# Moving six sums and differences of a 3x3 convolution's first two groups from VectorE to GpSimd

## The chip, the cores and the metric

The kernel runs on one core of one Trainium2 chip. A core has engines that run side by side, each through its own queue of instructions in order: TensorE (PE) multiplies matrices into PSUM, VectorE (DVE) and ScalarE (ACT) work element by element and can read PSUM, GpSimd (POOL) works element by element on SBUF, and SyncE (SP) issues transfers; ACT and GpSimd issue some transfers too. Engines wait for one another through semaphores. The metric is the device time of one execution in microseconds, less is better.

## The reference

Two bottleneck blocks, one after the other, on an input of 64 images of 1024 channels and 14 by 14 pixels, all in fp32:

```python
out = jax.nn.relu(_bn(_conv(x, w1, b1, 1, 0), g1, be1))      # 1x1, 1024 -> 256
out = jax.nn.relu(_bn(_conv(out, w2, b2, 1, 1), g2, be2))    # 3x3, 256 -> 256
out = _bn(_conv(out, w3, b3, 1, 0), g3, be3)                 # 1x1, 256 -> 1024
out = jax.nn.softplus(residual_scale)[0] * out
return jax.nn.relu(x + out)
```

Batch norm takes mean and variance over all 64 images, so each convolution must be finished before its result can be normalized.

## The kernel before

The 256 channels between the convolutions lie in one SBUF tile, `y_all`, for all images; `y_grp` is a view of it by groups of 8 images. The 1x1 convolutions use a fast matrix multiplication with seven products in place of eight. Each block has one 3x3 stage (`conv2`), and the change is in it alone. In the profile these stages lie at about 305 to 560 us and 1258 to 1540 us.

The 3x3 stage works through `NG` = 8 groups of 8 images. Within a group the 14 rows are cut in `RT` = 4 tiles of 4 output rows (the last tile has 2), and each tile of rows is computed from `NF` = 6 products by a fast convolution along the rows, made in pairs in the order (1, 2), (3, 4), (5, 0). I number these products 0 to 47 through a stage, six to a group. Per product the work is:

- DVE makes combinations of input rows, `steps` and `r`, and from each of them the column sums, differences and steps `sums`, `diffs`, `v` (`combine`, `Inputs`, lines 667, 681, 689, 760 to 784, and 636 for every multiply-and-add).
- TensorE multiplies them with transformed filters: `m` from the sums, `l` from the differences, and even and odd `columns` from the steps (line 175).
- ACT copies `m` into both halves of the `columns` bank pair before TensorE adds its columns to them (`put`, lines 844, 846, or 338 where the order is written out; below: the fill), and `l` into the SBUF tile `ls` (`bring`, line 866 or 338).
- DVE adds `columns` and `ls` into a tile `f` (`add_to`, line 885; below: the eviction).

TensorE's order in step k is: `l` of k, even columns of k, `m` of k + 1, odd columns of k. There are two `columns` bank pairs of PSUM, so the fill of product k + 1 waits for the eviction of product k - 1, and the even columns of k + 1 wait for that fill.

`finish` makes the output rows from the six evictions of a group. From the first two it makes the sum `a` (tile `fa`) and the difference `d` (tile `fb`); from the next two the sum `c` (tile `fc`) and the difference `e`, written over the older of the two `f` tiles. ACT copies the last row of each from `a` and `d` into `y` (lines 939 and 946). The inner rows come from these four by multiply-and-adds on DVE (line 636, written `y<-f,fb` where it reads `e` and `d`, and `y<-fc,fa`), the first of the outer rows by an add on DVE (line 938). For groups 0 to 5 the remaining evictions, 4 and 5 of the group, are added to the output rows by transfers from GpSimd's queue (lines 965, 966 and 982); until those have landed, their `f` tiles stay taken. There are three `f` tiles and one each of `fa`, `fb`, `fc`.

A planner orders the instructions of each engine by its own estimates, except those passed to `keep_in_program_order` (TensorE's all are; ACT's are where `act` is called). So a changed engine can change the order of other instructions on DVE and ACT. In the compiled program of the changed kernel TensorE's and SyncE's orders are the same as before; DVE's and ACT's differ inside the 3x3 stages.

Of the kernel before, what the change touches and what calls it, by code (L numbers as in the profile page):

```python
# [90 lines left out]
def bottlenecks(ctx: ExitStack, tc: tile.TileContext, x, w1s, w2s, w3s, pars, out):  # L91
    nc = tc.nc
# [501 lines left out]
    def conv2(b, par, aff, early, rest):  # L594
# [32 lines left out]
        def new(tag, tiles=RT):  # L627
            v = place(tag, MS * RT * LINE)
            return v[:, : MS * tiles * LINE].rearrange("p (s r l) -> p s r l", s=MS, r=tiles)
# [5 lines left out]
        def stt(to, a, by, c):  # L635
            return nc.vector.scalar_tensor_tensor(to, a, by, c, ALU.mult, ALU.add)
# [253 lines left out]
        def halves(f):  # L890

            return f.rearrange("p o r (i q c) -> p q (o r i) c", i=GI, q=2)

        def outputs(c):
            return c.add_to(new("f", c.lines // GI))

        def finish():


            for g in range(NG):  # L900
                out_rows = [y_grp[:, :, g, k::4, :] for k in range(4)]
                last_group = g == NG - 1

                by_transfer = g < NG - 2

                def stat(k, lines):
                    if last_group:
                        for o in range(MS):
                            nc.vector.bn_stats(stats[:, o, 1 + k, :], lines[o])

                ca = yield
                fa = outputs(ca)
                if g == 1:
                    begin(y_grp[:, :, 0, 1 : 4 * full : 4, :])
                fb = outputs((yield))
                a, d = new("fa"), new("fb")
                nc.vector.tensor_add(a, fa, fb)
                nc.vector.tensor_sub(d, fa, fb)

                fa = outputs((yield))  # L920
                fb = outputs((yield))
                c, e = new("fc", full), fa
                nc.vector.tensor_add(c, fa, fb)
                nc.vector.tensor_sub(e, fa, fb)
                a3, d3 = (v[:, :, :full] for v in (a, d))
                end = y_grp[:, :, g, H - 1]

                def middle_rows():

                    for o in range(MS):  # L930
                        stt(out_rows[1][:, o, :full], e[:, o], 2.0, d3[:, o])
                        stt(out_rows[2][:, o], c[:, o], 4.0, a3[:, o])

                def outer_rows():

                    if by_transfer:

                        nc.vector.tensor_add(out_rows[0][:, :, :full], a3, c)
                        nc.scalar.activation(out_rows[0][:, :, full], a[:, :, full], AF.Copy)
                    else:  # L940
                        nc.vector.tensor_add(a3, a3, c)
                    if by_transfer:

                        for o in range(MS):
                            stt(out_rows[3][:, o], e[:, o], 8.0, d3[:, o])
                        nc.scalar.activation(end, d[:, :, full], AF.Copy)
                    else:
                        stt(d3, e, 8.0, d3)

                if g > 1:  # L950
                    middle_rows()
                    outer_rows()
                if last_group:
                    for o in range(MS):
                        lines = y_grp[:, o, g, 1 : 1 + 4 * full].rearrange("p (r k) l -> p r k l", k=4)[:, :, :2]
                        for k in range(2):
                            moment(lines, idle[:, : 2 * full * LINE].rearrange("p (r k l) -> p r k l", k=2, l=LINE), o, k, g)

                fa = outputs((yield))
                if g < 2:  # L960
                    outer_rows()

                if by_transfer:
                    for o in range(MS):
                        nc.gpsimd.dma_start(out=out_rows[3][:, o], in_=fa[:, o, :full], accum_op=ALU.add)
                    nc.gpsimd.dma_start(out=end, in_=fa[:, :, full], accum_op=ALU.add)
                else:
                    nc.vector.tensor_add(out_rows[3], d3, fa[:, :, :full])
                    nc.vector.tensor_add(end, d[:, :, full], fa[:, :, full])
                stat(0, [out_rows[3][:, o] for o in range(MS)])  # L970
                stat(1, [end[:, o] for o in range(MS)])
                if last_group:
                    merge()

                cb = yield
                if g < 2:
                    middle_rows()
                if by_transfer:

                    f = outputs(cb)  # L980
                    for o in range(MS):
                        nc.gpsimd.dma_start(out=out_rows[0][:, o], in_=f[:, o], accum_op=ALU.add)
                    continue
                nc.vector.tensor_add(halves(a), halves(a), cb.by_columns(cb.ls))
                for j, q in enumerate((EVEN, ODD)):
                    for o in range(MS):
                        to, more = (
                            v[:, o].rearrange("p r (i q c) -> p q r i c", i=GI, q=2)[:, q] for v in (out_rows[0], a)
                        )
                        nc.vector.tensor_add(to, cb.banks[:, q, o].rearrange("p (r i c) -> p r i c", r=RT, c=WH), more)  # L990
                    stat(2 + j, [out_rows[0][:, o].rearrange("p r (i q c) -> p q r i c", i=GI, q=2)[:, q] for o in range(MS)])
            yield
# [8 lines left out]
        def begin(lines):  # L1001

            for o in range(MS):
                act(idle[:, : full * LINE].rearrange("p (r l) -> p r l", l=LINE), lines[:, o], AF.Identity,
                    scale=-1.0 / (full * LINE), accum_out=center[:, o : o + 1])

        def moment(y, to, o, k, g):
            act(to, y, (AF.Identity, AF.Square)[k], bias=center[:, o : o + 1], accum_out=moments[:, o, k, g : g + 1])

        def merge():  # L1010

            n = GPX * (NG - 1) + 2 * full * LINE
            m = small.tile([P, MS, 2], FP, tag="m12", name="m12")
            for o in range(MS):
                nc.vector.tensor_reduce(m[:, o], moments[:, o], mybir.AxisListType.X, ALU.add)
            eng = nc.gpsimd
            eng.tensor_scalar(m, m, 1.0 / n, None, ALU.mult)
            var = small.tile([P, MS], FP, tag="m12var", name="m12var")
            eng.tensor_tensor(var, m[:, :, 0], m[:, :, 0], ALU.mult)
            eng.tensor_sub(var, m[:, :, 1], var)  # L1020
            eng.tensor_sub(m[:, :, 0], m[:, :, 0], center)

            for half in range(2):
                to = stats[:, :, 0, 3 * half : 3 * half + 3]
                eng.memset(to[:, :, 0], n / 2)
                eng.tensor_copy(to[:, :, 1], m[:, :, 0])
                eng.tensor_scalar(to[:, :, 2], var, n / 2, None, ALU.mult)
# [29 lines left out]
        for _ in first_combination(inputs, 0, t):  # L1057
            pass
        coming, finished = items(), finish()
        next(finished)  # L1060

# [674 lines left out]
```

## Time and profile before

| what | us |
|---|---|
| median of three runs (1921.5 to 1921.92) | 1921.75 |
| the profiled execution | 1921.91 |
| its span, first to last instruction | 1920.1 |
| TensorE busy | 1902.8 |
| DVE busy | 1544.7 |
| ACT busy | 1086.5 |
| GpSimd busy | 564.6 |
| one of the 16 sums `fa`, or differences `fb`, 128 x 896, on DVE | 1.09 |
| one of the 16 sums `fc`, or differences in an `f` tile, 128 x 672, on DVE | 0.85 |
| DVE busy between 305 and 353 us, 48 us | 47.34 |

Times in profile lines are microseconds from the span's start. In a line of the timeline the first number is the start, the second the duration, then come the engine, the line of the kernel, the operation, the output and input tiles and their sizes; brackets give the idle time of the engine before the instruction and what ended it. Consecutive instructions on DVE overlap by some 0.08 us in the records. The stages are not alike: what an engine is worth in the 3x3 stage is read there and not from its share of the whole span.

### The profile page before, as it was taken

To read this page: it belongs to the slowest core of one execution; us is meant where nothing else is said; L and a number is where in the kernel's file an instruction comes from. 1 tells how busy PE (TensorE), PEld (TensorE's weight loads), DVE (VectorE), ACT (ScalarE), POOL (GpSimd) and SP (SyncE) were. 2 spreads that over 40 slices of the span, in tenths; PEclk is the share of its full clock that TensorE was granted. 3 is DMA by queue.
4 is the path that set the end of the run, shared out by engine and by line. 5 is a ranking of instruction groups with operands and counts; after the bars stand their busy time and mean duration, and the time that the engine had idled before them with its cause. 6 is when DMAs were issued, how large, how long until landed. Compare 5 with 4: busy or idle time off the path is not lost.

```text
span 1920.1 us, 28731 instructions
## 1 busy us (share of the span) xinstructions
PE 1902.8 (99%) x10236; PEld 1598.6 (83%) x10236; DVE 1544.7 (80%) x2499; ACT 1086.5 (57%) x2160; POOL 564.6 (29%) x678
## 2 busy tenths in 40 slices
PE   9999999999999999999999999999999999999999
PEld 5555557999998799999999999989999987555555
DVE  5787767999998866676776767789999986888886
ACT  2222214677778255555555555556777682666666
POOL 0111100211204133433433333302121041666664
PEclk9999999999999999999999999999999999999999
DMA  7767644887856544444444444358878466899998
GB/s 291 272 245 272 221 156 154 204 214 212 215 169 172 193 159 169 169 168 181 178 180 168 168 169 178 124 179 208 213 207 223 141 171 243 291 325 346 328 338 303
DMA packets 198527, 408.77 MB, mean 213 GB/s; under 512 B 37104, under 2 KB 175024, under 8 KB 181872
## 3 DMA queue, kind: packets, MB, share of 16 engines
q1 hardware_dynamic: 159712, 321.85, 48.9%
q0 software_dynamic: 33056, 34.03, 8.5%
q10 hardware_dynamic: 5616, 51.06, 6.4%
q8 instruction: 81, 1.33, 0.3%
q14 instruction: 62, 0.51, 0.1%
HBM read 263.75 MB, written 115.34 MB: 197 GB/s over the span
## 4 chain that ended last, share of the span: by engine, by line
PE 87%; issue 5%; DVE 3%; DMA 2%; POOL 2%; ACT 1%; SPq 0%; DVEq 0%; POOLq 0%; ACTq 0%
PE cy L175 17%; PE ay L175 14%; PE columns L175 14%; PE cp L175 11%; PE ap L175 8%; PE m L175 7%; PE l L175 6%; PE cx L175 5%; PE ax L175 4%; PE ps L175 1%; POOL home L1186 1%; POOL u L222 1%; DMA home<-y 1%; DVE zt L1223 0%; DMA u<-y 0%
## 5 line engine op out<-in xcount | busy, mean ns | idle before, releaser
L338 ACT ACTIVATE cu<-cy,scale 128x196 f32<-128x196 f32 (+1 forms) x552 | 256.3, 473 | 278.1 <-PE cy L175 272.9
L175 PE MATMUL columns<-v,ub 128*128 128x224 f32 (+1 forms) x1536 | 302.6, 339 | 4.8 <-ACT columns L846 3.9
L338 ACT ACTIVATE x<-x,shift 128x392 f32<-128x392 f32 x452 | 255.0, 613 | 73.1 <-POOL x L530 53.9
L175 PEld LDWEIGHTS columns<-v,ub 128*128 128x128 f32 x1536 | 269.0, 189 | 10.8 <-ACT columns L846 5.8
L504 DVE SCALAR_TENSOR_TENSOR x<-cp,scale,x 128x196 f32<-128x196 f32 (+1 forms) x368 | 178.3, 484 | 96.4 <-PE cp L175 95.2
L175 PE MATMUL cy<-ct,ws 128*128 128x196 f32 (+1 forms) x736 | 222.0, 383 | 1.2 <-ACT cu L338 1.2
L175 PE MATMUL ay<-at,ws 128*128 128x196 f32 (+1 forms) x768 | 212.9, 382 | 0.0
L525 POOL TENSOR_TENSOR x<-x,cu 128x196 f32<-128x196 f32 (+1 forms) x184 | 159.6, 867 | 171.6 <-ACT cu L338 163.8
L530 POOL TENSOR_TENSOR x<-x,cu 128x392 f32<-128x392 f32 x124 | 125.8, 1014 | 191.8 <-DVE x L504 186.9
L175 PEld LDWEIGHTS ay<-at,ws 128*128 128x128 f32 x768 | 139.5, 190 | 34.7 <-ACT au L338 0.6
L175 PEld LDWEIGHTS cy<-ct,ws 128*128 128x128 f32 x736 | 133.6, 190 | 36.2 <-ACT cu L338 3.7
L175 PE MATMUL l<-diffs,ub 128*128 128x224 f32 (+1 forms) x768 | 149.6, 337 | 0.3 <-ACT sd L1478 0.3
L551 POOL TENSOR_TENSOR x<-x,cu 128x392 f32<-128x392 f32 x120 | 121.9, 1016 | 86.4 <-DVE x L504 63.0
L175 PE MATMUL m<-sums,ua 128*128 128x224 f32 (+1 forms) x752 | 146.0, 337 | 0.2 <-DVE sums L667 0.2
L338 ACT ACTIVATE au<-ay 128x196 f32<-128x196 f32 (+1 forms) x140 | 53.3, 381 | 147.9 <-PE ay L175 145.4
L175 PEld LDWEIGHTS l<-diffs,ub 128*128 128x128 f32 x768 | 134.7, 190 | 1.1 <-ACT sd L1478 0.6
L504 DVE SCALAR_TENSOR_TENSOR x<-cx,scale,x 128x196 f32<-128x196 f32 (+1 forms) x184 | 89.1, 484 | 56.7 <-PE cx L175 56.5
L175 PEld LDWEIGHTS m<-sums,ua 128*128 128x128 f32 x752 | 131.5, 190 | 1.3 <-DVE sums L667 0.7
L175 PE MATMUL cy<-y,w 128*128 128x196 f32 (+1 forms) x408 | 125.4, 394 | 0.0
L175 PE MATMUL cx<-y,w 128*128 128x196 f32 (+1 forms) x400 | 122.7, 392 | 0.0
L175 PE MATMUL cp<-y,ws 128*128 128x196 f32 (+1 forms) x368 | 113.6, 391 | 0.1
L175 PE MATMUL cy<-ct,w 128*128 128x196 f32 (+1 forms) x368 | 111.0, 383 | 0.5 <-ACT cu L338 0.5
(238 smaller groups left out, 3915.2 us busy)
## 6 DMA issues: line engine op xcount, KB each, us to landing
x<-in_x SPq DMA_DIRECT2D x62, 1568.0 KB, 6.9
ub<-u SPq DMA_DIRECT2D x92, 768.0 KB, 5.4
x<-mid SPq DMA_DIRECT2D x32, 1568.0 KB, 7.9
mid<-x ACTq DMA_DIRECT2D x31, 1568.0 KB, 5.1
out<-x SPq DMA_DIRECT2D x123, 392.0 KB, 5.6
ua<-u SPq DMA_DIRECT2D x92, 256.0 KB, 3.0
u<-y POOLq DMA_DIRECT2D x48, 256.0 KB, 6.2
home<-y SPq DMA_DIRECT2D x70, 96.0 KB, 3.6
```

Of the source, the lines that this page charges most:

```text
L175: tc.keep_in_program_order(nc.tensor.matmul(*args, **kw))
L222: nc.gpsimd.dma_start(out=us[b][i][:, s, o], in_=u)
L338: tc.keep_in_program_order(nc.scalar.activation(*args, **kw))
L504: nc.vector.scalar_tensor_tensor(v, bank, self.scale[:, o : o + 1], v, ALU.mult, ALU.add)
L525: nc.gpsimd.tensor_add(self.part(1, 1), self.part(1, 1), u3)
L530: nc.gpsimd.tensor_add(v, v, self.u12)
L551: nc.gpsimd.tensor_add(v, v, self.u12[:, i * self.n : (i + 1) * self.n])
L1186: ins = queue.dma_start(out=x[32 * i : 32 * i + 32, :, j], in_=y_all[32 * j : 32 * j + 32, :, a + i * run : a + i * run + run])
```

## The change

In group 0 the sum `a`, the difference `d`, the sum `c` and the difference `e` are computed by GpSimd instead of DVE; in group 1 only `c` and `e` are. All other groups are as before. The stage is run once per block, so twelve instructions move.

```diff
                 fb = outputs((yield))
                 a, d = new("fa"), new("fb")
-                nc.vector.tensor_add(a, fa, fb)
-                nc.vector.tensor_sub(d, fa, fb)
+                eng = nc.vector if g else nc.gpsimd
+                eng.tensor_add(a, fa, fb)
+                eng.tensor_sub(d, fa, fb)

                 fa = outputs((yield))
                 fb = outputs((yield))
                 c, e = new("fc", full), fa
-                nc.vector.tensor_add(c, fa, fb)
-                nc.vector.tensor_sub(e, fa, fb)
+                eng = nc.vector if g > 1 else nc.gpsimd
+                eng.tensor_add(c, fa, fb)
+                eng.tensor_sub(e, fa, fb)
```

## The prediction

> **What bounds the kernel now.** I read the page's busy times first:
>
> ```profile
> PE 1902.8 (99%) x10236; PEld 1598.6 (83%) x10236; DVE 1544.7 (80%) x2499; ACT 1086.5 (57%) x2160; POOL 564.6 (29%) x678
> ```
>
> TensorE is busy 99% of the span, so a shorter vector queue can win only where TensorE waits for it. Next I asked what TensorE waited for in the first two groups of each 3x3 stage, 290 to 420 us and 1280 to 1410 us:
>
> ```profile
> PE columns L175 <- ACT columns L846: 1.6, 2, 1.1
> ...
> PE columns L175 <- ACT columns L846: 1.9, 2, 1.4
> ```
>
> Two waits in each block, 3.5 us in all: that is all there is to win here. The timelines of DVE, ACT and TensorE show what is late:
>
> ```profile
> 351.06 2.09 DVE L885 TENSOR_TENSOR f<-columns,ls 128x896 f32<-128x896 f32 x2
> ...
> 352.24 1.09 ACT L846 ACTIVATE columns<-m 128x448 f32<-128x448 f32 x2 [2.44 <-DVE f L885]
> ...
> 353.38 1.81 PE L175 MATMUL columns<-v,ub 128*128 128x224 f32 x8 [1.08 <-ACT columns L846]
> ```
>
> [...]Eviction 5 (first of the two at 351.06) frees the bank pair that ACT fills for product 7, and TensorE waits 1.08 us for that. The same happens 34 us later with eviction 11 (0.55 us), and in block 1 (1.38 and 0.55 us). The eviction's data had lain ready for 6.5 us (odd columns 5 end at 344.5): DVE is behind. From 314 to 356 us DVE never idles, so each us added to or taken from its queue ahead of eviction 5 moves that eviction by a us.
>
> Whether GpSimd takes the work off DVE without harm is read where both work today, in the 1x1 stages:
>
> ```profile
> 1007.27 0.60 POOL L525 TENSOR_TENSOR x<-x,cu 128x196 f32<-128x196 f32 x1
> 1009.14 1.35 POOL L525 TENSOR_TENSOR x<-x,cu 128x196 f32<-128x196 f32 x1 [1.27 <-ACT cu L338]
> ...
> 1009.05 0.97 DVE L456 TENSOR_TENSOR at<-x,at 128x784 f32<-128x784 f32 x1 [1.24 <-PE ay L175]
> ...
> 1641.24 1.13 POOL L525 TENSOR_TENSOR x<-x,cu 128x392 f32<-128x392 f32 x1
> ...
> 1641.42 1.37 DVE L470 TENSOR_TENSOR ct<-y 128x392 f32<-128x392 f32 x1
> 1642.71 0.55 DVE L468 TENSOR_TENSOR ct<-y 128x392 f32<-128x392 f32 x1
> ```
>
> The same GpSimd add takes 0.60 us alone and 1.35 us when it starts 0.09 us into a DVE add of two SBUF tiles; it ends 0.47 us (its own 0.60 less 0.13) after DVE's add. The other way round, DVE's L470 takes 1.37 us behind a running GpSimd add where its twin L468 takes 0.55; it really begins 0.13 us before GpSimd's end. They take turns.
>
> [...]this trace has 600 ns for 196 and 1015 for 392, or 0.185 us + 2.12 ns an element. At the sizes moved that is 2.08 us (896) and 1.61 us (672), estimates[...].
>
> **The change part by part, block 0.** In each block six instructions leave DVE: a and d of group 0 (896), c and e of groups 0 and 1 (672). Start to start these cost DVE 1.00 and 0.77 us (325.65 to 326.65; 335.39 to 336.16), so group 0 is relieved by 2.00 + 1.54 = 3.54 us, group 1 by 1.54.
>
> They reappear on GpSimd, which was idle there (34 us before 341.10), but beside two-SBUF adds. Which of two waiting engines gets the port between back-to-back DVE adds this trace doesn't show: I take alternation. Then, with the compiled order of the changed kernel:
> - Eviction 1 ends at 324.96 and a is released; DVE's r (324.88 to 325.73) holds the port, so a ends at 325.73 + 1.95 = 327.68. DVE's next, sums, begins at 327.55 and not 325.65: 1.9 us late. d ends 1.95 after sums (328.64), at 330.59, and DVE's diffs loses 1.9 us more.
> - Eviction 3 releases c. DVE's sums is ahead of it (1.0 us); c ends 1.48 us after that (2.48 after the eviction). DVE's next, the sum into y (L938), waits for c, and the one after it (L636, y from e) waits for e, which queues behind c and contends with L938. That one starts about 4.9 us after the eviction, where sums and L938 alone would have ended after 1.7: 3.2 us late.
>
> So DVE loses 1.9 + 1.9 + 3.2 = 7.0 us and is spared 3.54: it is 3.5 us later at eviction 5, which goes to about 354.5, and TensorE's columns 7 go from 353.38 to 356.9.
>
> An ACT queue effect lies under this. ACT runs in order, and the new order puts both last-row copies (L939 reading a, L946 reading d) ahead of the fill of the bank pair for product 3. Today:
>
> ```profile
> 326.83 0.39 ACT L939 ACTIVATE y<-fa 128x224 f32<-128x224 f32 x1
> 327.12 0.90 ACT L338 ACTIVATE columns<-m 128x336 f32<-128x336 f32 x2
> ```
>
> L946 can't start before d ends at 330.59, so the fill runs 330.95 to 331.85 and TensorE's columns 3, today at 328.52, start at 331.9: a 3.4 us stall. It doesn't add to the 3.5: TensorE, 3.4 late, would reach columns 7 at 355.7, and DVE's 356.9 decides.
>
> Group 1 adds 3.2 and spares 1.54 (+1.7), but now uses up the 1.84 us for which DVE waits for TensorE before eviction 7 (at 357.99). Eviction 11: 3.5 + 1.7 - 1.8, 3.4 us late, taken as 3.3 with roundings. TensorE alone would be 3.5 late less the vanished wait of 0.55. So block 0 ends 3.3 us later.
>
> **Block 1.** The order differs: only L939 lies inside the fill of product 3 (one half before it, one after), L946 is ahead of fill 4. a ends at 1278.76 + 1.95 = 1280.7, today's L939 starts at 1280.82: no stall there. DVE loses the same 7.0 us, is spared 3.54; ACT's fill for product 7 is no longer split by an ls copy (0.3 us gained), and DVE's wait in group 1 is 2.17 us. Together 3.5 + 1.7 - 2.2 = 3.0 us.
>
> From group 2 on no instruction moves engine. DVE's order differs slightly and reaches in group 3 the order that the kernel before has from group 5, where TensorE doesn't wait: 0. GpSimd's queue: the transfers of row 3 (L965, L966) stand behind c and e, but wait for evictions 4 and 10 anyway (347.6 and later), after e: 0. They land 3 to 7 us after issue, before eviction 6 (358) wants their buffer, just; if not, up to 1 us more a block. The sync queue and TensorE's order are unchanged. In the copy of e into the old f tile one wait is added, for c: counted above.
>
> Sum: 3.3 + 3.0 = 6.3 us. The profiled execution took 1921.91 us (span 1920.1, 1.8 us around it), 0.16 above the median of 1921.75: 1928.2 on its scale, **1928.0** on the median's.
>
> **Bounds of the unknown.** If GpSimd gets the port only when DVE pauses or evicts, d ends after eviction 2 (about 333.1 in block 0): fill 3 ends at 334.4, a stall of 5.9 us. DVE itself loses 0.9 less, so TensorE decides, and the vanished waits of 1.08 and 0.55 come off: block 0 is 4.3 late, block 1 about 2: again 6.3. If even the short pause between dependent adds doesn't let it in, a waits for eviction 2 and d for eviction 3, and the blocks are about 8 and 3 late.
>
> **Rivals.**
> 1. *No blocking in this stage*: the 1x1 lines don't carry over, GpSimd runs beside DVE. Then DVE is early and the four waits for evictions 5 and 11 (1.08 + 0.55 + 1.38 + 0.55 = 3.56 us) go. In block 0, a and d still end at 327.1 and 329.2, L946 holds fill 3 until 330.5, 2.0 us of stall. Net -3.56 + 2.0 = -1.6: 1920.1. This is the one on the other side; it decides once less than 3.5 of the 7.0 us of DVE's losses are real. Against it: every overlap of such adds in the trace shows the block. 0.12, of which 0.03 beyond 0.2% (the stall at fill 3 missing too: 1918.2).
> 2. *Half hidden*: GpSimd's adds fall more beside evictions and DVE's waits than I laid them, lateness about 1.5 us a block: 1924.8. For it: evictions take 5.5 of a group's 33 us[...]. 0.16.
> 3. *Starved GpSimd*, as bounded above: L946 in ACT's queue makes columns 3 very late. 11 us: 1932.7. Against: dependent adds leave some 0.1 us between them. 0.12.
> 4. My forecast, 4 to 8.5 us slower: 0.60. Its own range is 1925.7 to 1930.2.
>
> That the change does nothing is out: GpSimd's compiled queue has 12 instructions more.
>
> **Range and chances.** 0.2% (3.8 us) is about what can be told from no change. Slower: 0.60 + 0.12 = 0.72; same: 0.16 + 0.09 = 0.25; faster 0.03. From 1921.5 (leaves out most of rival 1) to 1932.5 (half of rival 3).
>
> **What would show it.** GpSimd's rows of 896 elements at 2.1 us alone, near 2.7 to 4 with waits; DVE's sums and diffs in group 0 near 3 us instead of 1.09; ACT waiting for GpSimd before L939 and L946; TensorE's wait before columns 3 of block 0 of about 3.4 us, and none in block 1; waits for fill 7 still there. If DVE's adds keep 1.09 us, rival 1 holds. Wrong also if TensorE waits in groups 2 to 7, which I put at nothing.

## The result, and the profile after

The changed kernel takes 1936.41 us (five runs, 1935.57 to 1937.44) against 1921.75 us (five runs by then, 1921.5 to 1921.92): a ratio of 1.0077 with a 95% interval of 1.0067 to 1.0088. It is slower by 14.7 us. The forecast was 1928.0 us with a range up to 1932.5: the direction was right, the size was less than half of what came.

The page's busy times of the changed kernel show first that no engine became the bound:

```profile
PE 1906.0 (99%) x10236; PEld 1597.6 (83%) x10236; DVE 1544.6 (80%) x2487; ACT 1087.4 (56%) x2160; POOL 594.8 (31%) x690
```

DVE has twelve instructions less and is as long busy as before (1544.7 us): what it was spared came back as longer instructions. TensorE's busy time grew by 3.2 us for the same matmuls. Most of the loss must then be waits of TensorE. These are its waits in the first groups of the two stages (290 to 420 and 1280 to 1410 us; total, number, longest):

```profile
PE columns L175 <- ACT columns L338: 3.6, 2, 3.1
PE columns L175 <- ACT columns L846: 3.1, 2, 2.6
PE columns L175 <- ACT columns L844: 0.9, 1, 0.9
...
PE columns L175 <- ACT columns L846: 3.9, 3, 2.6
PE columns L175 <- ACT columns L844: 2.4, 2, 1.6
PE m L175 <- DVE sums L667: 1.4, 2, 0.7
```

Before, there were two waits for fills of line 846 in each block, 3.5 us in all. Five lines of the kernel before, for comparison: DVE's sums and diffs behind eviction 1, TensorE's columns 3, and columns 13 with their fill:

```profile
326.65 1.09 DVE L667 TENSOR_TENSOR sums<-r 128x896 f32<-128x896 f32 x1
...
329.42 1.09 DVE L689 TENSOR_TENSOR diffs<-r 128x896 f32<-128x896 f32 x1
...
328.52 1.31 PE L175 MATMUL columns<-v,ub 128*128 128x168 f32 x8
...
386.67 1.09 ACT L846 ACTIVATE columns<-m 128x448 f32<-128x448 f32 x2 [2.45 <-DVE f L885]
...
387.81 1.80 PE L175 MATMUL columns<-v,ub 128*128 128x224 f32 x8 [0.55 <-ACT columns L846]
```

The timeline of the changed kernel shows what is late in block 0. Line numbers are up to two higher than before (a and d are now lines 918 and 919, c and e 925 and 926, the copies of the last rows 941 and 948, the sum into y 940):

```profile
325.89 2.57 POOL L918 TENSOR_TENSOR fa<-f 128x896 f32<-128x896 f32 x1 [18.46 <-DVE f L885]
328.43 2.92 POOL L919 TENSOR_TENSOR fb<-f 128x896 f32<-128x896 f32 x1
...
326.62 2.79 DVE L667 TENSOR_TENSOR sums<-r 128x896 f32<-128x896 f32 x1
329.34 2.96 DVE L689 TENSOR_TENSOR diffs<-r 128x896 f32<-128x896 f32 x1
...
331.38 0.39 ACT L948 ACTIVATE y<-fb 128x224 f32<-128x224 f32 x1 [2.49 <-POOL fb L919]
331.67 0.90 ACT L338 ACTIVATE columns<-m 128x336 f32<-128x336 f32 x2
...
332.62 2.06 PE L175 MATMUL columns<-v,ub 128*128 128x168 f32 x8 [3.15 <-ACT columns L338]
334.47 2.75 PE L175 MATMUL m<-sums,ua 128*128 128x224 f32 x8
...
341.85 0.86 DVE L940 TENSOR_TENSOR y<-fa,fc 128x672 f32<-128x672 f32 x1 [1.50 <-POOL fc L925]
344.21 0.93 DVE L636 SCALAR_TENSOR_TENSOR y<-f,fb 128x336 f32<-128x336 f32 x2 [1.51 <-POOL f L926]
...
355.58 1.08 DVE L885 TENSOR_TENSOR f<-columns,ls 128x896 f32<-128x896 f32 x1
...
392.68 0.53 ACT L846 ACTIVATE columns<-m 128x448 f32<-128x448 f32 x1 [2.45 <-DVE f L885]
394.71 0.39 ACT L633 ACTIVATE r<-y 128x224 f32<-128x224 f32 x1 [1.51 <-DVE v L681]
395.01 0.53 ACT L846 ACTIVATE columns<-m 128x448 f32<-128x448 f32 x1
...
395.58 1.80 PE L175 MATMUL columns<-v,ub 128*128 128x224 f32 x8 [2.57 <-ACT columns L846]
```

The first four lines show the turns: DVE's sums and diffs, 1.09 us before, take 2.79 and 2.96, and GpSimd's two adds lie between them. (The prediction and the expectations speak of a port: that is my word for what makes the two engines take turns. The traces show the turns and not their cause.) Then ACT stands before its copy of d, fill 3 behind it is late, and TensorE waits 3.15 us before columns 3. The next two lines are DVE's waits for c and e. All this was forecast. The last four lines were not: fill 13, whose halves stood together before, is done with the r of line 633 between its halves, and that waits for DVE; TensorE waits 2.57 us before columns 13. Other waits in the list were not forecast either: 0.85 us before columns 12 in both blocks and 1.56 us before columns 6 in block 1 (line 844), and two for DVE's sums in block 1 (1.4 us).

To see where the time goes, I followed how much later TensorE starts each product than before, counted from the first matmul of the stage. There are two steps: up to columns 7, and from there to columns 15. The table collects the experiments too. What a half clock of TensorE cost on the way (told below) is taken off in them; in the changed kernel's profile there was one, in block 0, nearly hidden in the first step (a run told below with the same order up to there and no half clock there, the first attempt on fill 13, is 3.6 us late at columns 7):

| us that TensorE loses | block 0 to columns 7 | block 0, columns 8 to 15 | block 1 to columns 7 | block 1, columns 8 to 15 |
|---|---|---|---|---|
| predicted | 3.5 | -0.2 | 3.2 | -0.2 |
| the changed kernel | 3.8 | 3.8 | 3.1 | 4.0 |
| GpSimd does the sums, order of before | 2.3 | 1.3 | 3.1 | 1.3 |
| DVE does the sums, order of the changed kernel | 0.3 | 2.4 | 0.0 | 1.7 |
| only group 1's c and e on GpSimd, order of before | 0.0 | 1.3 | 0.0 | 1.3 |

The first step came out as predicted. The second, 7.8 us, is what the prediction missed: it put it at slightly less than nothing. The table's row for the changed kernel sums to 14.7 us, while the profiled execution is 13.7 us longer than that of the kernel before: outside these steps two profiles differ by up to 1.3 us either way, so that totals agree no better than to about 1 us.

One line more, from the busy times by stretches of time of the changed kernel (length, the engines' busy time, then PEclk, the granted clock of TensorE):

```profile
core 0: us, PE busy (x) PEld busy (x) DVE busy (x) ACT busy (x) POOL busy (x), PEclk, DMA share, GB/s
333.26:336.68 3.42, 3.42 (x12) 3.24 (x11) 3.32 (x5) 2.68 (x6) 0.00 (x0) 0.50 0.00 0
336.70:340.00 3.30, 3.30 (x21) 3.30 (x20) 3.27 (x4) 1.87 (x5) 0.57 (x1) 1.00 0.31 85
```

From 0.6 us after the wait before columns 3 TensorE runs at half clock for about 3.4 us (PEclk 0.50 from 333.26 to 336.68). Columns 3 take 2.06 us and not 1.31, m of product 4 takes 2.75 and not 1.68.

### The profile page after: what moved, and what is told of

Same layout as the page of the kernel before. It is cut to its first block, busy times and chain, and to the rows that moved or that the text cites. A ratio compares the mean times of both kernels' runs of the same rounds, so it can differ in the third digit from the quotient of the medians.

```text
span 1933.8 us, 28743 instructions
## 1 busy us (share of the span) xinstructions
PE 1906.0 (99%) x10236; PEld 1597.6 (83%) x10236; DVE 1544.6 (80%) x2487; ACT 1087.4 (56%) x2160; POOL 594.8 (31%) x690
## 4 chain that ended last, share of the span: by engine, by line
PE 83%; issue 7%; DVE 6%; POOL 2%; DMA 1%; ACT 1%; SPq 0%; POOLq 0%; DVEq 0%; ACTq 0%
PE cy L175 17%; PE ay L175 14%; PE cp L175 12%; PE columns L175 10%; PE ap L175 9%; PE m L175 5%; PE l L175 5%; PE cx L175 5%; PE ax L175 4%; PE ps L175 1%; DVE steps L768 1%; DVE v L681 1%; DVE f L885 1%; POOL u L222 1%; DVE diffs L689 1%
```

## The experiments

My theory after the result (A): DVE and GpSimd take turns, TensorE then waits for late evictions, and the new order of ACT and DVE adds waits of its own in the second step. Rivals: only GpSimd's work costs; only the order costs; only the wait for GpSimd's results costs.

To hold one thing while changing another, the order of DVE and ACT in groups 0 to 2 is written out by instruction number. The edges order instructions and add no semaphore. All the kernels share this edit; what changes is the list (the third kernel's has one pair a block). Each ratio is to runs of the kernel before made beside it, whose medians were 1921.5 to 1921.7 us:

```diff
+ORDERS = [
+    [(1517, 1505, 1506, 1548, ...), ...],
...
+def in_order(tc, chains):
+    by = {i.name: i for i in tc.nc.cur_bb.bb.instructions}
+    for chain in chains:
+        for first, then in zip(chain, chain[1:]):
+            tc.add_manual_dep(by[f'I-{then}'], f'I-{first}',
+                mybir.DependencyInfo(mybir.DependencyClass.NoSync, mybir.DependencyReason.DATA), reason='order')
...
-            border.go_on(Psum(scope, ["l"], l=2, m=2), pool, stats2)
+            border.go_on(Psum(scope, ["l"], l=2, m=2), pool, stats2); in_order(tc, ORDERS[b])
```

### Engine and order, one at a time

The first kernel has GpSimd do the sums in the order of before.

```diff
-nc.vector.tensor_add(a, fa, fb)
+(nc.vector if g else nc.gpsimd).tensor_add(a, fa, fb)
... (d, c and e as in the change)
+ORDERS: DVE and ACT as in the kernel before
```

> GpSimd does the twelve sums and differences, as in the changed kernel, but VectorE and ScalarE keep the order of the kernel before (the split fill 13, the fill behind the border copies and the adds' new neighbours are undone). Theory A (turns on the shared port and the waits for GpSimd's results cost, and the new order of ScalarE and VectorE costs on top): eviction 5 late by 2 to 2.5 us, group 1 adds 1 to 1.5 us, no wait at columns 13 for a split fill: +3.5 us a block, about 1929 us (1926.5 to 1931.5). Rival B (only the work on GpSimd costs; the order is without effect): as the changed kernel, about 1936 us. Rival C (only the order costs): as before, about 1922 us.

It took 1933.27 us (4 runs, 1929.97 to 1934.78; ratio 1.0059, 1.0042 to 1.0075), above A's range. The timeline says why. Its lines of TensorE and DVE, and the last of them in the kernel before:

```profile
355.27 1.81 PE L175 MATMUL columns<-v,ub 128*128 128x224 f32 x8 [2.50 <-ACT columns L846]
...
390.99 1.79 PE L175 MATMUL columns<-v,ub 128*128 128x224 f32 x8 [1.84 <-ACT columns L846]
...
1312.97 2.90 PE L175 MATMUL columns<-v,ub 128*128 128x224 f32 x8 [2.92 <-ACT columns L846]
...
359.87 1.09 DVE L885 TENSOR_TENSOR f<-columns,ls 128x896 f32<-128x896 f32 x1 [1.85 <-PE columns L175]
...
357.99 1.09 DVE L885 TENSOR_TENSOR f<-columns,ls 128x896 f32<-128x896 f32 x1 [1.84 <-PE columns L175]
```

Columns 7 come 2.34 us late, and group 1 adds 1.30 at columns 13: both as A expected. In block 1 it is 3.08 and 1.29, so 8.0 us in all, or about 1929.8 us. The one run whose mean clock is given as 1.000 took 1929.97. The profiled run has two half clocks in block 1 (columns 7 take 2.90 us there, not 1.81), which cost TensorE 1.65 and 1.67 us: 8.0 + 3.3 = 11.3, and its span is 11.4 us longer than before (closer than the 1 us or so to which such totals agree). So A was right in the waits and left out what a wait does to the clock. The last two lines are the important ones: before eviction 7 DVE still waits 1.85 us for TensorE (1.84 before), though it came 2.3 us late to this group.

The second kernel is the other half: DVE does everything, in the order of the changed kernel.

```diff
+ORDERS: DVE and ACT as in the changed kernel, DVE's six adds a block put in
```

> VectorE does all sums and differences, as before, but VectorE and ScalarE follow the order of the changed kernel (VectorE's adds put in where they stood). Theory A: the split fill 13 costs 1.9 us a block, the fill behind the border copies nearly nothing since sums and differences are there early: about 1925.7 us (1923 to 1927.5). Rival B (only GpSimd's work costs): 1921.8 us. Rival C (only the order costs): about 1936 us.

It took 1926.54 us (8 runs, 1924.6 to 1927.47; ratio 1.0023, 1.0013 to 1.0034), near A's number. Neither rival holds. Its lines of ACT and TensorE:

```profile
386.21 0.53 ACT L846 ACTIVATE columns<-m 128x448 f32<-128x448 f32 x1 [2.45 <-DVE f L885]
388.25 0.39 ACT L633 ACTIVATE r<-y 128x224 f32<-128x224 f32 x1 [1.51 <-DVE v L681]
388.54 0.53 ACT L846 ACTIVATE columns<-m 128x448 f32<-128x448 f32 x1
...
389.12 1.80 PE L175 MATMUL columns<-v,ub 128*128 128x224 f32 x8 [2.16 <-ACT columns L846]
...
399.86 1.42 PE L175 MATMUL columns<-v,ub 128*128 128x168 f32 x8 [0.54 <-ACT columns L846]
```

The order alone brings the split fill 13 and a wait of 2.16 us (0.55 before), and a new wait of 0.54 before columns 15. It costs 0.3 us or less up to columns 7.

### Group 1 by itself

```diff
-nc.vector.tensor_add(c, fa, fb)
-nc.vector.tensor_sub(e, fa, fb)
+(nc.gpsimd if g==1 else nc.vector).tensor_add(c, fa, fb)
+(nc.gpsimd if g==1 else nc.vector).tensor_sub(e, fa, fb)
+ORDERS: DVE and ACT as in the kernel before
```

> GpSimd does only the second group's c and e, VectorE everything else, all in the order of the kernel before. Theory A (group 1 costs by itself and additively, without the credit of 1.84 and 2.17 us of the prediction): the wait before columns 13 grows by 1.3 us in each block, as in the run with both groups in this order, and nothing else moves: about 1924.3 us (1923.3 to 1925.5). Rival (without group 0's lateness VectorE has its wait before eviction 7 as a reserve, so that group 1 alone costs nothing): 1921.8 us.

1925.21 us (20 runs, 1922.53 to 1928.36; ratio 1.0017, 1.0011 to 1.0024). TensorE before columns 13 in the two blocks:

```profile
388.86 2.80 PE L175 MATMUL columns<-v,ub 128*128 128x224 f32 x8 [1.85 <-ACT columns L846]
...
1345.65 1.80 PE L175 MATMUL columns<-v,ub 128*128 128x224 f32 x8 [1.85 <-ACT columns L846]
```

This is within A's range. Both waits are 1.85 us where before they were 0.55: 1.30 more in each block, with or without a late group 0 ahead of it. The wait before eviction 7 is no reserve for it: it ends at 357.74 in this profile, and GpSimd's c of group 1, beside which DVE loses its time, starts only at 368.75. In block 0 a half clock follows (2.80 us for the columns) and in block 1 none: same wait, different luck, and the wide spread of the times.

### The split fills

The third kernel was to join fill 13 in the changed kernel by moving line 633 alone behind it.

```diff
 ACT, both blocks:
 columns<-m L846 (fill 13, first half)
-r<-y L633
 columns<-m L846 (fill 13, second half)
+r<-y L633
```

> The changed kernel with one instruction of ScalarE's queue moved in each block: the r of line 633 stands behind the second half of fill 13 instead of between the halves. Theory A (the split is worth 1.9 us a block): 1936.4 less 3.8, about 1932.6 us (1931.5 to 1934). Rival (the late second half is covered: columns 13 would wait as long for VectorE's eviction 11): 1936.4 us, no change.

1936.11 us (4 runs, 1935.27 to 1936.95; ratio 1.0076, 1.0061 to 1.0091), no change, but it tests nothing. Between the halves of fill 13, at 390.94 and 393.27, ACT now has (numbers of the kernel before):

```profile
392.97 0.39 ACT L781 ACTIVATE r<-y 128x224 f32<-128x224 f32 x1 [1.51 <-DVE v L681]
```

The planner put the r of line 781 into the gap, and that waits for the same v. So I held the whole order of the changed kernel and made the same move:

> The changed kernel with VectorE's and ScalarE's whole order of these groups held as it is, but the r of line 633 put behind both halves of fill 13 in each block (in the earlier attempt the r of line 781 took its place between them). Theory A (the split keeps TensorE waiting 1.9 us before columns 13): the wait before columns 13 falls from 2.57 to about 0.7 us in both blocks, 1936.4 less 3.8, about 1932.5 us (1931 to 1934). Rival (the late second half is covered by VectorE's lateness at eviction 11): the wait stays near 2.5 us and the time at 1936.

1935.20 us (4 runs, 1934.34 to 1936.1; ratio 1.0071, 1.0057 to 1.0085): 1.2 us gained where 3.8 were expected, and the runs overlap with the changed kernel's. In the lines of TensorE and ACT:

```profile
393.73 1.80 PE L175 MATMUL columns<-v,ub 128*128 128x224 f32 x8 [0.80 <-ACT columns L846]
...
404.93 0.39 ACT L939 ACTIVATE y<-fa 128x224 f32<-128x224 f32 x1 [1.99 <-DVE fa L917]
405.23 0.43 ACT L846 ACTIVATE columns<-m 128x336 f32<-128x336 f32 x1
...
405.71 1.42 PE L175 MATMUL columns<-v,ub 128*128 128x168 f32 x8 [1.58 <-ACT columns L846]
```

The wait before columns 13 fell from 2.57 to 0.80 as A said, but the one before columns 15 grew from 0.53 to 1.58, since fill 15 is split too, around the copy of a, and a did not come earlier. At columns 15 TensorE is 0.5 us less late in each block. Then both splits were joined, in the changed kernel and in the one where DVE does the sums in the changed order:

```diff
 ACT, both blocks, with r<-y L633 moved as above:
 columns<-m L846 (fill 15, first half)
-y<-fa L939
 columns<-m L846 (fill 15, second half)
+y<-fa L939
```

> The changed kernel with fills 13 and 15 both joined in each block (the r of line 633 behind fill 13, the border copy of a of line 939 behind fill 15; else its own order). With fill 13 alone joined, 1.05 us of the 1.77 us saved before columns 13 came back before columns 15, where fill 15 waits in halves for VectorE's sum a. Theory A (the two splits are what group 1's order costs): the wait before columns 15 falls from 1.58 to under 0.3 us in both blocks, 1935.2 less 2 times 1.3 to 1.7, about 1932.2 us (1931 to 1933.5). Rival (the lateness shows again at a later columns product): 1934.5 to 1935.5 us.

> VectorE does all sums and differences in the order of the changed kernel (1926.5 us), with fills 13 and 15 joined as in the other run of this pair. Theory A (the two splits are nearly all that the new order costs): about 1922.5 us (1921.5 to 1923.7). Rival (VectorE's own new order, a late eviction 11, costs it): 1925 us or more.

They took 1933.77 us (4 runs, 1932.59 to 1935.16; ratio 1.0063, 1.0048 to 1.0078) and 1924.19 us (20 runs, 1922.91 to 1925.02; ratio 1.0012, 1.0005 to 1.0019), both a little above A's ranges. TensorE in the first of them:

```profile
393.75 1.79 PE L175 MATMUL columns<-v,ub 128*128 128x224 f32 x8 [0.80 <-ACT columns L846]
...
422.73 1.62 PE L175 MATMUL columns<-v,ub 128*128 128x224 f32 x7 [1.07 <-ACT columns L844]
```

Joining both takes 2.6 us off the changed kernel and 2.4 off the other: the waits before columns 15 are gone, but a wait of 1.07 us before columns 18 appears in both blocks, behind a late eviction, as the rival said in part. From columns 7 to past that wait TensorE loses 0.9 us a block less than with the splits (for the second kernel this can be read in block 0 alone, since in block 1 the run with the splits has a half clock). The rest of the 2.4 to 2.6 us fits half clocks that no longer follow the waits of 2.57 and 2.16 us (the mean clock is given as 1.000 in 17 of the 20 runs of the second kernel, and in 2 of the 8 runs that have the splits), but no run shows that by itself. And the second kernel is still 2.5 us slower than the kernel before: the two splits are about half of what the order costs, and the rest shows mostly before columns 18.

### The turns by themselves

GpSimd gets four adds of its own in group 0 of each block; their results go to a spare tile that nobody reads. DVE and ACT keep all their work and their order.

```diff
-                nc.vector.tensor_sub(d, fa, fb)
+                nc.vector.tensor_sub(d, fa, fb); other_work(g, a, d)
...
+        def other_work(g, a, d):
+            for s, op in itertools.product(range(MS), (nc.gpsimd.tensor_add, nc.gpsimd.tensor_sub) * (g == 0)):
+                op(pool.tile([P, RT * LINE], mybir.dt.bfloat16, tag="other", name="other")
+                    .rearrange("p (r l) -> p r l", r=RT), a[:, s], d[:, s])
```

> The kernel before, in its order, with four GpSimd additions (two sums, two differences of 448 elements) of a and d added in group 0 of each block, whose results nobody reads and nobody waits for. Theory A (the shared port alone delays VectorE's two-input instructions from SBUF, which take turns with GpSimd's): each of the four GpSimd additions holds up one VectorE instruction by 0.6 to 1.1 us, eviction 5 comes 2.5 to 4 us late, TensorE waits that much longer before columns 7, about 1928.5 us (1926 to 1932). Rival B (the cost of the change is that its readers wait for GpSimd's slower results): no effect, 1921.8 us.

1927.41 us (5 runs, 1926.67 to 1929.64; ratio 1.0031, 1.0019 to 1.0043), within A's range. The lines of GpSimd and DVE:

```profile
328.16 7.42 POOL L899 TENSOR_TENSOR other<-fa,fb 128x448 bf16<-128x448 f32 x4 [22.19 <-DVE fb L919]
...
328.76 1.50 DVE L689 TENSOR_TENSOR diffs<-r 128x896 f32<-128x896 f32 x1
330.19 2.69 DVE L681 TENSOR_TENSOR v<-r 128x1536 f32<-128x1536 f32 x1
332.80 3.50 DVE L636 SCALAR_TENSOR_TENSOR steps<-y 128x672 f32<-128x672 f32 x2
```

Before, these DVE instructions took 1.09, 1.76 and 1.62 us: 0.41 + 0.93 + 1.88 = 3.2 us lost, while DVE was kept from no result. TensorE is 3.26 us late at columns 7 in block 0 and 2.53 in block 1. So the turns cost by themselves; the rival that only the wait for results costs is out. The multiply-and-adds of line 636, which have two SBUF inputs as well, take turns like the adds (3.50 us for the two here, 1.62 before).

### The wait and the clock

The kernel with only group 1 on GpSimd again, but the eight matmuls of one l product in each block are done twice (TensorE's order around them is written out as well).

```diff
-                to = self.bank(tag)
-                for o, s in each:
+                to = self.bank(tag); made["whole"] += 1
+                for o, s in each * (1 + (made["whole"] == 22)):
```

> The kernel with only group 1's c and e on GpSimd (1925.2 us), and in each block the eight matmuls of the l product directly ahead of columns 13 done a second time, with the same result: TensorE has 3.4 us more work, in the place where it waited 1.85 us. If the wait itself brings on the half clock that was seen behind such waits (about 1.7 us lost each time), there is none now: the wait before columns 13 is 0.2 to 0.4 us, the clock stays full in all runs, and the time is that of the runs without a half clock, 1923.9 us (1923.2 to 1924.7), with a smaller spread. Rival (the half clock has another cause): again 1925.2 us or more, with the same spread from 1922.5 to 1928.4 us; and 1927 us or more if the repeated product delays ScalarE's copy of it.

The repeated product turned out to be the l of product 12, directly ahead of columns 12, and not the one directly ahead of columns 13. Its time still comes out of the same wait, since nothing between them waits (block 1 has 0.35 us):

```profile
388.32 1.80 PE L175 MATMUL columns<-v,ub 128*128 128x224 f32 x8 [0.34 <-ACT columns L846]
```

1923.73 us (13 runs, 1922.7 to 1924.8; ratio 1.0012, 1.0003 to 1.0020) against 1925.21 us with less work. Columns 13 start as late as there (1.3 us behind the kernel before), so the 1.5 us are put down to the half clocks that no longer follow: the profile has none in these stages. The spread shrinks from 5.8 to 2.1 us. The intervals of the two ratios overlap, but 12 of the 20 runs without the repeated product are slower than the slowest of the 13 with it.

### Evictions 5 and 11 earlier

If VectorE's lateness at two evictions is what TensorE waits for, moving these two forward must help the kernel before.

```diff
 DVE, for eviction 5 of both blocks (eviction 11 alike):
 steps<-y L768
 y<-f,fb L636
 r<-steps L636 (two)
+f<-columns,ls L885 (eviction 5)
 y<-fc,fa L636
 sums<-r L667
 y<-f,fb L636
 y<-fc,fa L636
-f<-columns,ls L885 (eviction 5)
 f<-columns,ls L885 (eviction 6)
```

> The kernel before, with evictions 5 and 11 of each block put ahead of the last border sums (four instructions of VectorE earlier, directly behind the second r of line 636). If VectorE's lateness at evictions 5 and 11 is what TensorE waits for before columns 7 and 13 in the kernel before (1.08 + 0.55 + 1.38 + 0.55 = 3.56 us), about 1918.2 us (1917.5 to 1919.5). Rival (the delayed border sums and sums of the next group make TensorE or ScalarE wait elsewhere): 1921.8 us or more.

1918.42 us (20 runs, 1916.96 to 1920.22; ratio 0.9986, 0.9979 to 0.9992), as expected. Of the four waits only one of 1.07 us was left, before columns 7 of block 1, where ACT copies half of an l product between the halves of fill 7. In the next kernel these halves stand together:

```diff
 ACT, block 1:
 columns<-m L846 (fill 7, first half)
-ls<-l L866
 columns<-m L846 (fill 7, second half)
+ls<-l L866
```

> The kernel before with evictions 5 and 11 four instructions earlier, as in the earlier run (1918.4 us), and in block 1 the second half of fill 7 directly behind the first (before, a copy of an l product stood between). If the 1.07 us wait left before columns 7 of block 1 came from that copy, 1917.4 us (1916.5 to 1918); otherwise 1918.4 us.

1917.34 us (13 runs, 1915.96 to 1919.9; ratio 0.9978, 0.9969 to 0.9986): this kernel is faster than the kernel before and than the changed kernel. The eviction that was at 351.06 now starts at 348.94, and no wait for a fill of line 846 is left in groups 0 to 2.

Last, the same order with the twelve sums on GpSimd:

```diff
-nc.vector.tensor_add(a, fa, fb)
+(nc.vector if g else nc.gpsimd).tensor_add(a, fa, fb)
... (d, c and e as in the change)
```

> GpSimd does the twelve sums and differences as in the changed kernel, the order is that of the kernel before with evictions 5 and 11 four instructions earlier and the second half of fill 7 joined in block 1. Theory A (what TensorE waits for is VectorE's lateness at evictions 5 and 11): the four waits of 2.50, 1.84, 2.92 and 1.85 us shrink by some 1.9 us each, without half clocks, about 1922.5 us (1921 to 1925). Rival (waits for GpSimd's results set the time): no change against the run in the order of before, 1930 to 1933 us.

1924.93 us (15 runs, 1923.74 to 1926.71; ratio 1.0018, 1.0010 to 1.0025), at the upper edge of A's range and far from the rival. In block 0 (290 to 420 us) the waits of TensorE for fills are down to small ones:

```profile
PE columns L175 <- ACT columns L846: 1.0, 3, 0.5
PE columns L175 <- ACT columns L338: 0.7, 2, 0.4
```

So the long waits of TensorE were DVE's lateness at evictions 5 and 11, and the half clocks came with them. But the move did not become much cheaper. The kernel is 3.3 us slower than the kernel before, and 7.6 slower than the same order with the sums on DVE; in the profiles TensorE has lost 7.1 us to that move by product 22, where in the order of before it lost 8.0 without half clocks. That loss is spread over many small waits, in block 1 partly for DVE's sums (1.0 us), and no run takes it apart.

## Why the prediction was right or wrong

**Turns of DVE and GpSimd: right.** I took alternation: DVE 1.9 + 1.9 + 3.2 us late. Measured: sums 1.70 and diffs 1.87 longer, and 1.50 + 1.51 us of waits for c and e. The turns come also where nobody waits for GpSimd: in the run with idle adds diffs take 1.50 us, 1.09 before. That evictions, with one SBUF input, would not lose time beside GpSimd was an assumption of the prediction. In the run with idle adds one that starts at 328.00 takes 0.85 us, as in the kernel before, though GpSimd's first add starts at 328.16. In the 1x1 stages of the kernel before an instruction with inputs of the same kind, line 504, takes 0.41 us at 1006.41, within GpSimd's add of line 530 (1006.29 to 1007.31), and 0.41 us at 1005.75, while GpSimd is idle.

**Eviction 5 and columns 7: right.** Predicted 3.5 and 3.2 us late, measured 3.8 and 3.1. TensorE's wait before columns 3 was to be 3.4 us in block 0 and none in block 1: 3.15 and none. In block 1 the lateness shows mostly one product earlier than I had it, 1.56 us before columns 6 and 0.77 before columns 7. That the wait before columns 3 "doesn't add to the 3.5" was nearly so, by a narrower margin than I had: the half clock behind it cost TensorE another 1.8 us (3.31 late at the start of columns 3, 5.08 before its odd columns), and TensorE and the fill were both ready for columns 7 at about 358.0.

**Group 1: this step failed.** It said that group 1 "now uses up the 1.84 us for which DVE waits for TensorE before eviction 7", and so gained back what it added. But that wait is for TensorE's columns 7, and these had been made late by the very lateness that I wanted to hide. Once TensorE has waited for DVE, both are late by the same amount, and DVE's later wait is as long as ever: 1.85 us in the run with the order of before. In the changed kernel's own order DVE idles 1.63 us there, behind eviction 6, for the r of line 782, which stands in ACT's queue behind fill 7, and fill 7 waited for eviction 5: the same cause again. Nor can a wait before eviction 7 take up what group 1 itself adds, since c and e come later. Group 1 by itself costs 1.3 us a block, with or without group 0 (both runs agree), not far from the 1.7 that I had before the credit.

**"From group 2 on ... 0": this failed too.** The instructions of group 2 stay on their engines, but in the new order fills 13 and 15 are split around ACT instructions that wait for DVE. I had compared where the instructions around fill 3 stood, and not those around the fills of group 2. The order alone costs 2.4 and 1.7 us in this step; joining the two splits takes 2.6 us off the changed kernel and about half off the cost of the order alone, and what is left shows mostly before columns 18, behind a late eviction, in a group where I had written 0. My reading from its trace, 1.9 us a block for fill 13 alone, was wrong as well: joined alone it made TensorE 0.5 us less late a block, because DVE's lateness came out at columns 15.

The two failed steps together make up 3.8 and 4.0 us where I had -0.2 and -0.2: 8.2 us, against a miss of 8.4; the profiles' totals, good to about 1 us, don't bear out so close an agreement. A term that I had left out altogether, the half clock, is in the times as well: the mean clock of the changed kernel's five runs is 0.996 to 0.999, that of the kernel before 1.000 or nearly so, and how much of the 14.7 us this is isn't shown. In the changed kernel the two steps interact (the 0.85 us before columns 12 is in neither of the runs that have one of them alone), so that the two causes can't be told apart there to a few tenths: 1.3 + 2.4 is 3.7 in block 0 (3.8 measured), 1.3 + 1.7 is 3.0 in block 1 (4.0 measured). In the run that has the 1.7 a half clock lies between columns 13 and 15 of block 1, and no wait is seen before columns 15, where block 0 has 0.54. In the first attempt on fill 13 it is the same: the block with a half clock there has no wait before columns 15, the other 0.54. So the wait, worth 0.7 us to block 0, is probably hidden; whether that is all of the missing 1.0 stays open.

**The rivals.** No blocking (1920.1) and half hidden (1924.8) are refuted by the durations. The starved GpSimd gave 1932.7, nearer to the time, but for the wrong reason: d ended at 331.35, as alternation has it (330.59, in a stage that starts 0.79 us later), and not at 333.1 or later.

## What to carry to other kernels

An idle time of an engine is a reserve only for lateness that arises ahead of it, and only if what it waits for isn't itself late for the same cause: before crediting it, ask whom the waited-for engine waited for. When an edit changes a planned order, read what now stands between the halves of every transfer or fill that a critical engine waits for, far past the edit, since one late eviction shows up again at the next wait until something absorbs it. And before moving work off an engine that is late at two known instructions, try to move those two instructions forward: here it gained 3.1 us, and 4.4 with one split fill joined, where moving the work lost 14.7.

## What the runs showed that I had not expected

TensorE's clock falls to half behind waits much shorter than I would have minded. In the profiled runs of all the kernels here TensorE waited 19 times for 1.84 to 3.15 us in these groups, and 9 times the clock was 0.5 afterwards: behind three of the five waits of 1.84 or 1.85 us, three of the ten of 2.16 to 2.92, and three of the four of 3.15. Behind the waits of up to 1.61 us it never was. Seven of the nine cost TensorE 1.65 to 1.8 us; two, at the wait of 3.15 us before columns 3, cost about 3.0, and there the half clock began before the wait was over. The one of these two that was read from its start, in the run with fill 13 joined, lasted some 6.8 us; five others, in four runs, lasted 3.4 us each. Waits of 1.84 and 1.85 us were enough three times, and the same wait of 1.85 us is followed by a half clock in one block and not in the other: no run here shows what decides that. Filling such a wait with repeated matmuls made a kernel 1.5 us faster (1923.73 against 1925.21 us).
